# Writing out the order of the first tiles: the opening of a four-stage transformer kernel on one Trainium2 core

## The chip, the cores and the metric

The kernel runs on one NeuronCore of a Trainium2 chip. A core has engines that work side by side, each through its own instructions in order: TensorE (PE in the profile; PEld is its weight load), VectorE (DVE), ScalarE (ACT), GpSimd (POOL) and SyncE (SP), which here only starts transfers. They signal each other with semaphores. The metric is the device time in microseconds of one execution, taken as the median of several runs.

## The reference

The computation has four stages over 2048 tokens (8 sequences of 256) with 512 features. Each stage normalises its input, computes something and adds it to its input:

1. a retention-like attention over the context, with four heads of 128,
2. a feed-forward part with ternary weights,
3. an mLSTM attention with 16 heads,
4. a mixture of 32 experts, of which each token uses four, and a shared expert.

The change concerns the beginning of the first stage. What it computes, cut to that:

```python
Q = jnp.einsum('bshd,hde->bshe', xh, Wh)      # xh: the normalised tokens, by head
K = jnp.einsum('bshd,hde->bshe', kh, Wh)      # kh = vh: the context, by head
V = jnp.einsum('bshd,hde->bshe', vh, Wh)
scores = jnp.einsum('bshe,bthe->bhst', Q, K) / jnp.sqrt(jnp.float32(hd))
masked = scores * Dn[None, :, :, :]
A = jnp.maximum(jnp.abs(masked.sum(axis=0)), 1.0)   # summed over the sequences
O = jnp.einsum('hst,bthe->bshe', A, V)
```

The scores are summed over all eight sequences before they are used, so nothing of `A` is known until the last token has been normalised and multiplied.

## The kernel before, in words

Tokens are worked on in 16 tiles of 128 (`NT`), four tiles to a chunk of 512 (`CH`). Everything of the change lies in `layer0_attention` (L245), before the gate.

SyncE starts the loads in a fixed order (L260 to L278): the head weights `Wh`, then per chunk four tiles `x` and the turned context `ctxT`, then the other weights and the decay table `dec`.

Q and K need not be formed one by one: Q K^T per head is x (Wh Wh^T) k^T. So the kernel makes `G = Wh Wh^T` once. TensorE turns `Wh` (`transpose_blocks`, L137, into the PSUM tile `pt`), ScalarE copies the result to `WhT` (L286), TensorE multiplies it into `pG` (L289), and ScalarE copies that to `G` (L291).

For each tile i there are these steps:

- `stats(i)`: VectorE takes mean and variance (L129, L130), ScalarE the root `sd` (L321).
- `normed(i)`: VectorE takes the reciprocal (L325) and writes `xn` (L327), TensorE transposes it in four blocks into `pt` (L137), ScalarE copies them to `xnT` (L329).
- `values(b, j)`: TensorE multiplies context and `Wh` into `pv` (L299), ScalarE copies it to `v` (L304). This is called for the first four half sequences here, and for the rest later.
- `queries(c, h)`: TensorE multiplies a chunk of `xnT` by `G` into `pq` (L333), VectorE copies it to `q` (L335).
- `scores(c, h, q)`: TensorE adds q k^T to one of four PSUM sums `s0` to `s3` (L342, L343). Those sums were opened with a matmul of zeros (L315), after a memset of `zero` (L312).

`pt` (the tag "t") and `pv` (which shares its tag with `pG`) have one buffer each, so a transpose waits until the tile before was copied, and the first `pv` waits until `G` was copied. `xn` has two buffers.

The loop over n runs `stats` one tile ahead, `queries` four steps behind, `scores` five. In the steps 6 to 11 `ternary.add()` puts sums over the second stage's weights `wst` on ScalarE (L196). In this part no order is written by hand: the tile framework's scheduler places each instruction on its engine's queue. From the gate on (`gate`, L365), a block `tc.manual_schedule(engines=...)` keeps the written order for the engines that it names.

Of the kernel before, what the change touches and what calls it, by code (L numbers as in the profile page):

```python
# [19 lines left out]
F32 = mybir.dt.float32  # L20
# [10 lines left out]
P = 128  # L31
# [5 lines left out]
NT = T // P  # L37
CH = 512
NCH = T // CH
H0 = 4  # L40
HD0 = 128
# [84 lines left out]
def norm_stats(g, mv, x):  # L126

    st = g.small.tile([P, 6], F32, tag="st", name="st")
    g.nc.vector.bn_stats(st, x)  # L129
    g.nc.vector.bn_aggr(mv, st)  # L130


def transpose_blocks(g, pool, src, n, dtype, ident, tag):

    pt = pool.tile([P, n, P], dtype, tag=tag, name="pt")
    for k in range(n):
        g.nc.tensor.transpose(pt[:, k, :], src[:, k * P : (k + 1) * P], ident)  # L137
    return pt
# [106 lines left out]
def layer0_attention(g, tc, cp, qpool):  # L245


    nc = g.nc
# [4 lines left out]
    with ExitStack() as ctx:  # L253
        wp = ctx.enter_context(tc.tile_pool(name="a0w", bufs=1, reuse_waits="tile"))
        work = ctx.enter_context(tc.tile_pool(name="a0work", bufs=2, reuse_waits="tile"))
        ps = ctx.enter_context(tc.tile_pool(name="a0ps", bufs=1, space=PSUM, reuse_waits="tile"))


        Wh = wp.tile([P, H0, HD0], F32, tag="Wh", name="Wh")
# [22 lines left out]

        WhT = work.tile([P, H0, HD0], F32, tag="wyT", name="WhT")
        nc.scalar.copy(WhT, transpose_blocks(g, ps, Wh.rearrange("p h e -> p (h e)"), H0, F32, g.ident, "t"))  # L286
        pG = ps.tile([P, H0, HD0], F32, tag="pv", name="pG")
        for h in range(H0):
            nc.tensor.matmul(pG[:, h], lhsT=WhT[:, h], rhs=WhT[:, h], start=True, stop=True)  # L289
        G = wp.tile([P, H0, HD0], F32, tag="G", name="G")  # L290
        nc.scalar.copy(G, pG)  # L291

        V = {}

        def values(b, j):
            c, o = divmod(b * S + j * P, CH)
            pv = ps.tile([P, D], F32, tag="pv", name="pv")
            for h in range(H0):
                nc.tensor.matmul(  # L299
                    pv[:, h * HD0 : (h + 1) * HD0], lhsT=g.ctxT[c][:, h, o : o + P], rhs=Wh[:, h, :],  # L300
                    start=True, stop=True,
                )
            vj = work.tile([P, D], F32, tag=f"v{j}", name=f"v{j}")
            nc.scalar.copy(vj, pv)  # L304
            V.setdefault(b, []).append(vj)
# [3 lines left out]


        zero = work.tile([P, S + P], BF16, tag="zero", name="zero", bufs=1)
        nc.vector.memset(zero, 0.0)  # L312
        sums = [ps.tile([P, S + P], F32, tag=f"s{h}", name=f"s{h}") for h in range(H0)]
        for h in range(H0):
            nc.tensor.matmul(sums[h], lhsT=zero[:, :P], rhs=zero, start=True, stop=False)  # L315

        def stats(i):
            mv = g.small.tile([P, 2], F32, tag="mv", name="mv")
            norm_stats(g, mv, g.X[i])
            sd = g.small.tile([P, 1], F32, tag="sd", name="sd")  # L320
            nc.scalar.activation(sd, mv[:, 1:2], AF.Sqrt, bias=g.eps["ln"])  # L321
            return mv, sd

        def normed(i, mv, sd):
            nc.vector.reciprocal(sd, sd)  # L325
            xn = work.tile([P, D], F32, tag="y", name="xn")
            nc.vector.tensor_scalar(xn, g.X[i], mv[:, 0:1], sd, ALU.subtract, ALU.mult)  # L327
            c, o = divmod(i * P, CH)
            nc.scalar.copy(xnT[c][:, :, o : o + P], transpose_blocks(g, ps, xn, KD, F32, g.ident, "t"))  # L329

        def queries(c, h):
            pq = ps.tile([P, CH], F32, tag="pq", name="pq", bufs=2)
            nc.tensor.matmul(pq, lhsT=G[:, h, :], rhs=xnT[c][:, h, :], start=True, stop=True)  # L333
            q = work.tile([P, CH], F32, tag="wy", name="q")
            nc.vector.tensor_copy(q, pq)  # L335
            return q

        def scores(c, h, q):
            for o in range(0, CH, S):
                last = c == NCH - 1 and o == CH - S  # L340
                k = g.ctxT[c][:, h, o : o + S]
                nc.tensor.matmul(sums[h][:, :S], lhsT=k[:, :P], rhs=q[:, o : o + S], start=False, stop=False)  # L342
                nc.tensor.matmul(sums[h][:, S:], lhsT=k[:, P:], rhs=q[:, o + P : o + S], start=False, stop=last)  # L343

        of, q = {0: stats(0)}, {}
        for n in range(NT + H0 + 1):
            if n + 1 < NT:
                of[n + 1] = stats(n + 1)  # L350
            if n < NT:
                normed(n, *of.pop(n))
            if 0 <= n - H0 < NT:
                q[n - H0] = queries(*divmod(n - H0, H0))
            if 0 <= n - H0 - 1:
                scores(*divmod(n - H0 - 1, H0), q.pop(n - H0 - 1))
            if n < 4:
                values(*divmod(n, 2))
            elif 6 <= n < 12:
                ternary.add()  # L360
# [61 lines left out]
        po, y, pw, wy, wyT, pz, raw = ({} for _ in range(7))  # L422
        E_ = mybir.EngineType
# [1382 lines left out]
@with_exitstack  # L1806
def layers_kernel(ctx: ExitStack, tc: tile.TileContext, args):
    g = Ctx()
    g.nc = tc.nc
    for name, ap in args.items():  # L1810
        setattr(g, name, ap)
    setup(g, ctx, tc)
    dr = ctx.enter_context(tc.tile_pool(name="dram", bufs=1, space=DRAM))
    g.vc_d = dr.tile([T, D], F32, tag="vc_d", name="vc_d")

    g.h_d = dr.tile([T, D + E], F32, tag="h_d", name="h_d")
    g.parts_d = dr.tile([2, 3, P, S], BF16, tag="parts_d", name="parts_d")
    with tc.tile_pool(name="ctxT", bufs=1, reuse_waits="tile") as cp, ExitStack() as both:
        with tc.tile_pool(name="wq", bufs=1, reuse_waits="tile") as qp:
            layer0_attention(g, tc, cp, qp)  # L1820
            sp = ctx.enter_context(tc.tile_pool(name="f1early", bufs=1, side="right", reuse_waits="tile"))
            load_early(g, sp)
            wp = both.enter_context(tc.tile_pool(name="a1w", bufs=1, side="right", reuse_waits="tile"))
            gates = Gates(g, wp)
            layer1_constants(g, wp)
            layers_joined(g, tc, qp, gates)
    layer1_ffn(g, tc)
# [60 lines left out]
```

## Time and profile before

| what | value |
|---|---|
| median of 3 runs | 1054.01 us (1052.76 to 1054.70) |
| the profiled execution's own time | 1053.98 us |
| its span | 1051.8 us |
| TensorE busy | 998.3 us, 95% |
| VectorE, ScalarE, GpSimd busy | 532.3, 404.9, 394.3 us |
| first matmul of the loop over tiles (transpose of tile 0) | at 11.64 us |
| first matmul of the gate | at 60.36 us |

In lines of the timeline the first number is the start in microseconds from the span's start, the second the length; then engine, line, operation, output and inputs by the program's names with their shapes, and the count of instructions merged into the row. In brackets stand the engine's idle time before the row and what ended it. A line of the table by stretch has the stretch, its length, TensorE's busy time with the count of instructions, the granted clock as a share of full speed, the share of the DMA engines and their GB/s.

### The profile page before, as it was taken

What the parts mean: (1) busy time and instruction counts of PE and PEld (TensorE: products, weight loads), DVE (VectorE), ACT (ScalarE), POOL (GpSimd) and SP (SyncE); (2) the same over time, 40 slices, a digit from 0 to 9 for tenths busy, and PEclk for the clock granted to TensorE, in tenths of its full rate; (3) what the DMA queues carried; (4) which work ended last, traced back from release to release, by engine and by line L of the source; (5) the groups of instructions that cost most, each with busy time, mean ns of one, the idle gap of its engine ahead of it and who ended that gap; (6) DMA issues with size and microseconds to landing.
All of it is one profiled execution on the core that took longest, in us unless ns stands there. A gap on an engine that the chain in (4) does not pass through costs nothing.

```text
span 1051.8 us, 14757 instructions
## 1 busy us (share of the span) xinstructions
PE 998.3 (95%) x5210; PEld 607.5 (58%) x5210; DVE 532.3 (51%) x1417; ACT 404.9 (38%) x692; POOL 394.3 (37%) x452
## 2 busy tenths in 40 slices
PE   6999999979999899998998999999999999999994
PEld 5766666534444356665443445556666667778772
DVE  6546566679997768787828942112112121212120
ACT  4453443447687757876321001221222222221211
POOL 0023443450000114888203045554555556454522
PEclk9999999999999999999899999999999999999997
DMA  9663433323421411241112447777777778899972
GB/s 344 229 208 135 142 108 136 110 56 60 72 57 39 90 38 48 69 137 39 50 60 91 160 145 194 176 194 189 190 206 208 204 210 231 215 246 236 245 192 36
DMA packets 101011, 152.41 MB, mean 145 GB/s; under 512 B 39576, under 2 KB 42264, under 8 KB 100892
## 3 DMA queue, kind: packets, MB, share of 16 engines
q1 hardware_dynamic: 81984, 106.78, 32.4%
q0 software_dynamic: 18944, 44.60, 19.2%
q8 instruction: 43, 0.70, 0.3%
q14 instruction: 40, 0.33, 0.1%
HBM read 110.42 MB, written 32.96 MB: 136 GB/s over the span
## 4 chain that ended last, share of the span: by engine, by line
PE 74%; DVE 13%; POOL 4%; ACT 3%; issue 3%; DMA 1%; SPq 0%; POOLq 0%; DVEq 0%; ACTq 0%
PE po L1638 14%; PE pg L1621 13%; PE pu L1621 13%; PE pw L365 5%; PE pz L400 5%; PE pt L1678 3%; PE p L1118 2%; PE pgu L990 2%; DVE ct L779 2%; PE py L1165 2%; DVE h L1131 1%; PE pv L299 1%; DVE am L1135 1%; PE s L342 1%; PE pq L333 1%
## 5 line engine op out<-in xcount | busy, mean ns | idle before, releaser
L1626 DVE TENSOR_TENSOR act<-pu,sg 128x264 f32<-128x264 f32 (+22 forms) x68 | 31.9, 469 | 313.2 <-PE pu L1621 313.2
L1663 POOL DMA_INDIRECT xg<-h_d,tok_of x85 | 83.4, 981 | 197.9 <-DVE of L1673 64.8
L1682 POOL DMA_INDIRECT out_x<-eo,to x85 | 133.0, 1564 | 55.1 <-ACT eo L1720 34.4
L1638 PE MATMUL po<-w,act 128*128 128x512 f32 (+10 forms) x456 | 143.1, 489 | 0.0
L1621 PE MATMUL pg<-xT,w 128*128 128x216 f32 (+21 forms) x512 | 134.8, 406 | 0.8 <-issue 0.8
L1720 ACT ACTIVATE eo<-po,slotw 128x512 f32<-128x512 f32 (+10 forms) x114 | 65.6, 576 | 177.0 <-PE po L1638 170.6
L1621 PE MATMUL pu<-xT,w 128*128 128x216 f32 (+21 forms) x512 | 133.3, 403 | 0.0
L1621 PEld LDWEIGHTS pg<-xT,w 128*128 128x128 f32 x512 | 93.2, 190 | 33.2 <-issue 17.8
L1621 PEld LDWEIGHTS pu<-xT,w 128*128 128x128 f32 x512 | 96.8, 190 | 26.2 <-issue 5.6
L1625 ACT ACTIVATE sg<-pg 128x264 f32<-128x264 f32 (+22 forms) x68 | 28.5, 419 | 202.9 <-PE pg L1621 178.8
L1118 PE MATMUL p<-wq,xqT 128*128 128x512 bf16 (+1 forms) x384 | 81.2, 361 | 7.0 <-DVE qi L1139 6.2
L1638 PEld LDWEIGHTS po<-w,act 128*128 128x128 f32 (+10 forms) x456 | 54.2, 154 | 57.4 <-issue 47.9
L386 POOL TENSOR_TENSOR y<-y,gam 128x512 f32<-128x512 f32 x16 | 20.2, 1265 | 138.8 <-DVE y L83 138.8
L1118 PEld LDWEIGHTS <-xqT 128*128 128x128 bf16 x384 | 37.2, 98 | 49.4 <-issue 12.5
L1679 DVE TENSOR_TENSOR xT<-pt,nw 128x512 f32<-128x512 f32 (+12 forms) x85 | 51.1, 601 | 20.5 <-PE pt L1678 20.5
L400 PE MATMUL pz<-wo,wyT 128*128 128x512 f32 x128 | 59.5, 609 | 1.3 <-ACT wyT L395 1.3
L365 PE MATMUL pw<-wg,xnT 128*128 128x512 f32 x128 | 57.8, 594 | 0.0
L1678 PEld LDWEIGHTS pt<-ident,xg 128*128 128x128 f32 (+15 forms) x340 | 39.1, 140 | 23.9 <-PE po L1638 10.5
L129 DVE BATCH_NORM_STATS2 st<-x 128x6 f32<-128x512 f32 x64 | 43.9, 686 | 12.0 <-POOL x L848 6.3
L1678 PE MATMUL pt<-ident,xg 128*128 128x128 f32 (+15 forms) x340 | 47.2, 260 | 0.7 <-DVE xT L1679 0.6
L779 DVE SCALAR_TENSOR_TENSOR ct<-pqk,xe 128x768 f32<-128x768 f32 x44 | 40.0, 951 | 8.4 <-PE pqk L775 7.9
L1165 PE MATMUL py<-wq,hq 128*128 128x512 bf16 x176 | 42.3, 391 | 1.7 <-DMA hq<-hq 1.7
(336 smaller groups left out, 1680.7 us busy)
## 6 DMA issues: line engine op xcount, KB each, us to landing
w<-in_w SPq DMA_DIRECT2D x32, 1024.0 KB
w<-in_w SPq DMA_DIRECT2D x32, 512.0 KB
wst<-in_w1T SPq DMA_DIRECT2D x8, 704.0 KB
wst<-in_w3T SPq DMA_DIRECT2D x8, 704.0 KB
wst<-in_w2T SPq DMA_DIRECT2D x6, 768.0 KB
x<-in_x SPq DMA_DIRECT2D x16, 256.0 KB
ctxT<-in_ctxT_d SPq DMA_DIRECT2D x4, 1024.0 KB
raw<-in_ctx SPq DMA_DIRECT2D x16, 256.0 KB
```

The costliest lines, as they stand in the source:

```text
L365: nc.tensor.matmul(pw, lhsT=xnT[c][:, k, o : o + P], rhs=wg[:, k, :], start=k == 0, stop=k == KD - 1)
L400: nc.tensor.matmul(pz[i], lhsT=wyT[i][:, k, :], rhs=wo[:, k, :], start=k == 0, stop=k == KD - 1)
L779: nc.vector.scalar_tensor_tensor(ct[:, r : r + 2, :], pqk[:, :, : S + P], 1.0 / math.sqrt(HD1), xe[:, r : r + 2, :], ALU.mult, ALU.mult,)
L1118: nc.tensor.matmul(both[:, m, : z - a], lhsT=xqT[:, k, :], rhs=w[:, k, a:z], start=k == 0, stop=k == KD - 1)
L1165: nc.tensor.matmul(py[t], lhsT=hqT[t][0][:, f, :], rhs=w2[:, f, :], start=f == 0, stop=f == NF - 1)
L1621: nc.tensor.matmul(pp[:, :n], lhsT=w[:, k, cols], rhs=xT[:, k, :n], start=k == 0, stop=k == KD - 1)
L1638: nc.tensor.matmul(po[h * at : h * at + n, :cols], lhsT=act[:, m, j * P : j * P + n], rhs=w[:, m, h * cols : (h + 1) * cols], start=m == 0 ...
L1663: nc.gpsimd.indirect_dma_start(out=xg[:n], out_offset=None, in_=h_d, in_offset=bass.IndirectOffsetOnAxis(ap=g.tok_of[:n, r, j : j + 1], ax ...
L1678: nc.tensor.transpose(pt[:, k, :n], xg[:n, k * P : (k + 1) * P], g.ident[:n, :n])
L1679: nc.vector.tensor_mul(xT, pt[:, :, :n], g.nw.unsqueeze(2).to_broadcast([P, KD, n]))
L1682: return nc.gpsimd.indirect_dma_start(out=g.out, out_offset=bass.IndirectOffsetOnAxis(ap=rows, axis=0), in_=eo, in_offset=None, compute_op ...
L1720: nc.scalar.activation(eo[:n, at : at + cols], po, AF.Copy, scale=w[r][:n, j : j + 1])
```

## The change

The memset, the zeroing matmuls, the making of `G`, the statistics and transposes of tiles 0 to 3 and the first two `values` are taken out of the scheduler's hands: they stand in a `manual_schedule` block for TensorE, ScalarE and VectorE, one tile after another. In this block `WhT` is copied before any root is taken, and `G` after the first tile's `xnT`. The loop starts at n = 2 and keeps what is left.

```diff
-        WhT = work.tile([P, H0, HD0], F32, tag="wyT", name="WhT")
-        nc.scalar.copy(WhT, transpose_blocks(g, ps, Wh.rearrange("p h e -> p (h e)"), H0, F32, g.ident, "t"))
-        pG = ps.tile([P, H0, HD0], F32, tag="pv", name="pG")
-        for h in range(H0):
-            nc.tensor.matmul(pG[:, h], lhsT=WhT[:, h], rhs=WhT[:, h], start=True, stop=True)
-        G = wp.tile([P, H0, HD0], F32, tag="G", name="G")
-        nc.scalar.copy(G, pG)
...
         zero = work.tile([P, S + P], BF16, tag="zero", name="zero", bufs=1)
-        nc.vector.memset(zero, 0.0)
         sums = [ps.tile([P, S + P], F32, tag=f"s{h}", name=f"s{h}") for h in range(H0)]
-        for h in range(H0):
-            nc.tensor.matmul(sums[h], lhsT=zero[:, :P], rhs=zero, start=True, stop=False)
+        WhT = work.tile([P, H0, HD0], F32, tag="wyT", name="WhT")
+        G = wp.tile([P, H0, HD0], F32, tag="G", name="G")
...
-        of, q = {0: stats(0)}, {}
-        for n in range(NT + H0 + 1):
-            if n + 1 < NT:
+        of, q = {}, {}
+        E_ = mybir.EngineType
+        with tc.manual_schedule(engines={E_.PE, E_.Activation, E_.DVE}):
+            nc.vector.memset(zero, 0.0)
+            for h in range(H0):
+                nc.tensor.matmul(sums[h], lhsT=zero[:, :P], rhs=zero, start=True, stop=False)
+            nc.scalar.copy(WhT, transpose_blocks(g, ps, Wh.rearrange("p h e -> p (h e)"), H0, F32, g.ident, "t"))
+            of[0] = stats(0)
+            pG = ps.tile([P, H0, HD0], F32, tag="pv", name="pG")
+            for h in range(H0):
+                nc.tensor.matmul(pG[:, h], lhsT=WhT[:, h], rhs=WhT[:, h], start=True, stop=True)
+            normed(0, *of.pop(0))
+            nc.scalar.copy(G, pG)
+            of[1] = stats(1)
+            normed(1, *of.pop(1))
+            values(0, 0)
+            of[2] = stats(2)
+            normed(2, *of.pop(2))
+            values(0, 1)
+            of[3] = stats(3)
+            normed(3, *of.pop(3))
+        for n in range(2, NT + H0 + 1):
+            if 3 <= n < NT - 1:
                 of[n + 1] = stats(n + 1)
-            if n < NT:
+            if 3 < n < NT:
                 normed(n, *of.pop(n))
```

In the program that it builds to, the order on SyncE and GpSimd is the same as before. On TensorE two places differ: the transposes of tile 1 stand in front of the first `pv`, and the third `pv` in front of the transposes of tile 3. ScalarE has one instruction more: an activation table load in front of `WhT`, before the one in front of the first root. ScalarE's sums over `wst` stand between the copies of tiles 12 to 15, where they came earlier or later before.

## The prediction

> **What bounds the kernel now.** I read the page's engine totals and chain first, then the timelines of TensorE, ScalarE and VectorE over the first 60 us, then busy time and granted clock by stretch.
>
> ```profile
> PE 998.3 (95%) x5210; PEld 607.5 (58%) x5210; DVE 532.3 (51%) x1417; ACT 404.9 (38%) x692; POOL 394.3 (37%) x452
> ...
> PE 74%; DVE 13%; POOL 4%; ACT 3%; issue 3%; DMA 1%; SPq 0%; POOLq 0%; DVEq 0%; ACTq 0%
> ```
>
> TensorE is busy for 95% of the span and carries 74% of the chain. What comes early or late before TensorE runs without a gap is therefore handed on to the end; DMA holds 1% of the chain, so nothing there waits to swallow it. The next view is TensorE's timeline (start, length, line, operation, count, and in brackets the idle time before it and what ended it).
>
> ```profile
> 3.76 1.09 PE L137 MATMUL pt<-ident,Wh 128*128 128x128 f32 x4 [0.83 <-DMA Wh<-in_Wh]
> 9.78 2.07 PE L289 MATMUL pG<-WhT 128*128 128x128 f32 x8 [4.93 <-ACT WhT L286]
> 11.64 1.06 PE L137 MATMUL pt<-ident,xn 128*128 128x128 f32 x4
> 12.87 2.08 PE L299 MATMUL pv<-Wh,ctxT 128*128 128x128 f32 x8 [0.17 <-ACT G L291]
> 14.74 1.05 PE L137 MATMUL pt<-ident,xn 128*128 128x128 f32 x4
> 15.63 1.16 PE L299 MATMUL pv<-Wh,ctxT 128*128 128x128 f32 x8
> 16.62 0.60 PE L137 MATMUL pt<-ident,xn 128*128 128x128 f32 x4
> ...
> 18.50 0.60 PE L137 MATMUL pt<-ident,xn 128*128 128x128 f32 x4
> ...
> 20.34 0.60 PE L137 MATMUL pt<-ident,xn 128*128 128x128 f32 x4
> ```
>
> I call the five transposes of `xn` T0 to T4. Their starts are 11.64, 14.74, 16.62, 18.50 and 20.34. After T4 the loop repeats every 2.60 us without a gap until the gate begins at 60.36, so T4's start is the number to predict. Two things set it: the 4.93 us before `pG`, and the slow first matmuls. A transpose takes 1.05 us until 14.74 and 0.60 from 16.62; eight passes of `pv` take 2.08 and then 1.16.
>
> ScalarE's timeline shows why `pG` waits: `WhT` stands behind four roots `sd`, of which the last waits for the fourth tile's statistics.
>
> ```profile
> 0.75 1.28 ACT L321 ACT_TABLE_LOAD   x1 [0.75 <-PEq L1876]
> 5.23 0.29 ACT L321 ACTIVATE sd<-mv,eps_ln 128x1 f32<-128x1 f32 x1 [3.20 <-DVE mv L130]
> ...
> 8.96 0.29 ACT L321 ACTIVATE sd<-mv,eps_ln 128x1 f32<-128x1 f32 x1 [0.50 <-DVE mv L130]
> 9.16 0.57 ACT L286 COPY WhT<-pt 128x512 f32<-128x512 f32 x1
> 12.05 0.30 ACT L321 ACTIVATE sd<-mv,eps_ln 128x1 f32<-128x1 f32 x1 [2.33 <-DVE mv L130]
> 12.26 0.56 ACT L291 COPY G<-pG 128x512 f32<-128x512 f32 x1
> ```
>
> The same roots run ahead of the tiles there, which is good for T1 to T4: the roots of four tiles are taken by 9.25, before TensorE wants the first. Last, TensorE's busy time and granted clock in four stretches of 3.41 us.
>
> ```profile
> 8.83:12.24 3.41, 2.46 (x11) 1.00 1.04 396
> 12.24:15.65 3.41, 3.24 (x16) 1.00 1.06 391
> 500.34:503.76 3.42, 2.52 (x17) 0.50 0.22 81
> 503.76:507.17 3.41, 3.41 (x11) 0.50 0.00 0
> ...
> 504.55 1.06 PE L877 MATMUL hT<-ident,yn 128*128 128x128 f32 x4
> ```
>
> At a granted 0.50 four transposes take 1.06 us, as T0 does, so the first 15 us ran at half clock although the column says 1.00 there. The clock rose after a stretch with 3.24 or 3.41 us of busy TensorE, and did not after 2.46 or 2.52. Fragmented work keeps it low.
>
> **The change part by part.** Handing from engine to engine costs 0.03 to 0.06 us in these rows (`WhT` ends at 9.73, `pG` starts at 9.78).
>
> *`WhT` in front of the roots.* The transposes of `Wh` end at 4.85 as before, `WhT` takes 4.89 to 5.46, `pG` 5.51 to 7.58: 4.27 us earlier. `pG` then waits for nothing and nothing waits for it but `G`.
>
> *A second table load.* In the built program a copy is now ScalarE's first operation and gets a table load of its own; the load for the root stands behind `WhT`, since it is a different set. It takes 1.28 us, with 0.02 before and 0.01 after it (one at 550.03 follows a result that ends at 550.02). It cannot be passed on an engine that works in order, so nothing excludes its full price: 5.48 to 6.76. Then sd0 0.30, reciprocal 0.15, `xn` 0.55 and handovers: T0 at 7.9, that is 3.7 us early. Price between 0 (if the order of loads were hidden) and 1.3 on T0; I take 1.3.
>
> The Trainium skill ("ScalarE: Activation LUTs", What ACT_TABLE_LOAD costs) puts a switch of sets at 1.28 us plus a drain of 1.38, which speaks against this change. The row at 561.90 shows the next activation 0.01 us after the load, with no drain; by the page's figure the forecast would be an estimated 1.4 us higher than mine.
>
> *The written ring.* On ScalarE the order becomes WhT, sd0, xnT0, G, sd1, xnT1, v, sd2, xnT2, v, sd3; on VectorE statistics, reciprocal and `xn` of a tile now stand together, so a root is not taken ahead any more. Each tile's root waits for the copies of the tile before. That is a wait added, and behind it on ScalarE stand every later copy, on VectorE every later statistic, on TensorE the next transpose. With the durations above:
> - T0 7.9 to 8.97, xnT0 to 9.6, G to 10.06 (the two overlap by 0.1), sd1 to 10.3, reciprocal and `xn` to 11.0: T1 at 11.1 (3.6 early).
> - `pv` of the first values follows T1 at 11.95. Its data are there: tile 4, loaded behind them, reached VectorE at 11.11. At half clock its result comes at 13.87; copy to 14.5, sd2 to 14.7, another 0.8 to `xn`: T2 at 15.5 (1.1 early). TensorE has idled for about 1.8 us.
> - Second `pv` 16.4 to 18.3, its copy to 18.9, then the third `pv` 19.0 to 20.8, which now stands in front of T3: T3 at 20.8 (2.3 late). sd3 and `xn` are hidden under that third `pv`.
> - The copy of the third values ends at 21.6, the fourth `pv` starts at 21.7.
>
> *The clock.* On the stretches of the profile, 12.24 to 15.65 now holds only about 1.8 us of work and 15.65 to 19.07 about 2.75. The last is 0.80 of the stretch; the rows bound the trigger between 0.74 and 0.95. If 0.80 is not enough, the clock rises at 22.48, T4 starts at 23.0, which is 2.65 us late. If it is, V and T run fast from 19.07 and T4 starts near 21.1: 0.8 late. With no rise at all before T4 it is 24.3: 4.0 late. From T4 both kernels run the same rows at the same 2.60.
>
> I do not know that the stretches lie the same way in every execution. Moving them through all positions with the same steps, T4 comes 2.6 to 4.4 us later than before's own T4, mean 3.5, if the trigger lies above 0.80; and between 0.1 earlier and 2.8 later, mean 1.5, if below. I take 3.2, between the profile's position and the mean, as the higher trigger is nearer to the only rows that fired (0.95 and 1.00).
>
> The Trainium skill ("TensorE: Matmul & The Clock Gate", What's actually happening) says that the gate looks at free-running windows of about 3.4 us and opens after a busy one. The four rows agree with the length; that the position is free no run here shows. By the page alone, with a fully busy window wanted, the mean of 3.5 would be the forecast.
>
> *Order of the later work.* ScalarE's sums of `wst` now stand between the copies of tiles 12 to 15. Each takes 1.57 us (1.38 and a read of 0.19), and TensorE has 1.4 us of slack per copy: one copy runs from 40.60 to 41.18, and the next transposes, which want its buffer, start at 42.56. The first two loads are there long before 43.68; the third comes about 4.2 us after the first sum ends, near 46.3, the fourth near 49, both before the copies behind them are due. I cost this at nothing; without that cover 0 to 1 us. The head's zeroing matmuls, the memset, and the queues of SyncE and GpSimd keep their order: 0.
>
> Sum: 1053.98 (the profiled execution, span 1051.8 and 2.2 around it; 0.03 under the median of the runs) + 3.2 = 1057.2 us.
>
> **Rivals.**
> - *Clock rises early, ring mostly hidden* (0.0 to 1.5 late): 0.80 of a stretch suffices. For: no row between 0.74 and 0.95 excludes it. Against: nothing fired below 0.95. 1054.0 to 1055.5, say 1054.8.
> - *Faster*: the mechanism is the 4.3 us gained on `pG`, kept through to T4. It decides if sd1 to sd3 do not wait for the copies in front of them, so that TensorE's own work is the only limit after 7.9: four transposes of 0.85 and four `pv` of 1.71 at half clock put T4 at 18.2, at full clock from 12.24 at 15.2, so about 17. Price 3 us: 1051. Against it stands the order itself: v copies in front of sd2 and sd3. It wins only if T3 starts before 18.50.
> - *The ring and a late stall*: the `wst` sums hold up the last copies by up to 1 us, or the table load drains: 1058 to 1059.
>
> **How the numbers follow.** Forecast (ring with a late clock, +2 to +4.4) 0.66; early clock 0.20; faster 0.05; ring and stall 0.09. A measurement of this kernel tells about 0.2%, 2.1 us. Slower by more: nine tenths of the forecast's 0.66, all of the 0.09, and a quarter of the early-clock case where the position is bad: 0.74. Faster 0.04. The rest, 0.22, is within. The range runs from the early-clock case's middle less half the spread of the runs shown (1052.76 to 1054.70) up to the stall case: 1054.2 to 1059.2.
>
> **What would show it.** `pG` near 5.5, a table load at about 5.48 in front of the first root, T1 near 11, an idle of 1.5 to 2 us before T2, T3 behind the third `pv` near 20.8 and T4 at 22.4 to 24.3; transposes of 1.05 us as late as T2 or T3; the gate 2 to 4 us later than 60.36, and the rest of the trace the same rows shifted. A T4 before 20.3, or T2's matmuls at 0.60 us, would prove me wrong, as would a gain or loss born after 62 us.

## The result, and the profile after

The changed kernel takes 1057.34 us (median of 15 runs, 1053.01 to 1058.28); the kernel before took 1054.01 us beside it (15 runs, 1051.73 to 1056.70). The ratio is 1.0027 with a 95% interval of 1.0018 to 1.0036: slower by 0.27%, or 3.3 us. The profiled execution took 1056.78 us, 2.80 more than before's; its span is 1054.8.

The page's engine totals and chain:

```profile
PE 1000.8 (95%) x5210; PEld 610.3 (58%) x5210; DVE 532.2 (50%) x1417; ACT 406.7 (39%) x693; POOL 394.2 (37%) x452
...
PE 70%; DVE 16%; POOL 5%; ACT 3%; issue 3%; DMA 1%; DVEq 0%; POOLq 0%; ACTq 0%
```

The 5210 matmuls are the same, but TensorE is busy for 2.5 us more (998.3 before). ScalarE has one instruction more, and 4 points of the chain have gone from TensorE, most of them to VectorE. TensorE's timeline of the changed kernel shows where:

```profile
3.74 1.09 PE L137 MATMUL pt<-ident,Wh 128*128 128x128 f32 x4 [0.81 <-DMA Wh<-in_Wh]
5.50 2.08 PE L348 MATMUL pG<-WhT 128*128 128x128 f32 x8 [0.67 <-ACT WhT L344]
7.99 1.08 PE L137 MATMUL pt<-ident,xn 128*128 128x128 f32 x4 [0.40 <-DVE xn L318]
11.30 1.09 PE L137 MATMUL pt<-ident,xn 128*128 128x128 f32 x4 [2.23 <-DVE xn L318]
12.18 1.91 PE L291 MATMUL pv<-Wh,ctxT 128*128 128x128 f32 x8
15.91 1.09 PE L137 MATMUL pt<-ident,xn 128*128 128x128 f32 x4 [1.82 <-DVE xn L318]
16.79 1.92 PE L291 MATMUL pv<-Wh,ctxT 128*128 128x128 f32 x8
19.38 2.08 PE L291 MATMUL pv<-Wh,ctxT 128*128 128x128 f32 x8 [0.68 <-ACT v L296]
21.25 1.06 PE L137 MATMUL pt<-ident,xn 128*128 128x128 f32 x4
22.13 1.83 PE L291 MATMUL pv<-Wh,ctxT 128*128 128x128 f32 x8
23.80 0.60 PE L137 MATMUL pt<-ident,xn 128*128 128x128 f32 x4
...
63.82 1.02 PE L376 MATMUL pw<-wg,xnT 128*128 128x512 f32 x2
```

`pG` starts at 5.50 instead of 9.78 and T0 at 7.99 instead of 11.64. Then each tile's `xn` is late: 2.23 us of idle time stand in front of T1 and 1.82 in front of T2. T2 starts only 0.71 us before its old place, T3 2.75 us behind it and T4 at 23.80, 3.46 late. Slow transposes (1.06 us) and slow `pv` (1.8 to 1.9 us) now start as late as 21.25 and 22.13; before, the clock rose at 15.65. The gate starts at 63.82, 3.46 late too: between T4 and the gate both kernels run the same work without a gap.

ScalarE's timeline of the changed kernel has the cause of the idle times:

```profile
0.75 1.28 ACT L344 ACT_TABLE_LOAD   x1 [0.75 <-PEq L1887]
4.87 0.58 ACT L344 COPY WhT<-pt 128x512 f32<-128x512 f32 x1 [2.84 <-PE pt L137]
5.47 1.28 ACT L312 ACT_TABLE_LOAD   x1
6.76 0.29 ACT L312 ACTIVATE sd<-mv,eps_ln 128x1 f32<-128x1 f32 x1
...
14.13 0.58 ACT L296 COPY v<-pv 128x512 f32<-128x512 f32 x1 [1.12 <-PE pv L291]
14.61 0.30 ACT L312 ACTIVATE sd<-mv,eps_ln 128x1 f32<-128x1 f32 x1
```

The second table load delays the first root to 6.76. The root of tile 2 (14.61) follows the copy of `v` (14.13), which waits for the `pv` that TensorE has just done; T2 waits for that root. TensorE and ScalarE take turns. How much of the delay is idle time and how much is slow work is read from TensorE's busy time by stretch (stretch, length, busy with the count of instructions, clock, DMA share, GB/s). Before, from the transposes of `Wh` to T4:

```profile
3.76:20.34 16.58, 10.95 (x61) 1.00 1.02 373
```

After, the same work, and two stretches of 3.41 us at its end:

```profile
3.74:23.80 20.06, 14.26 (x61) 1.00 1.02 377
...
16.74:20.15 3.41, 2.73 (x13) 1.00 1.05 387
20.15:23.56 3.41, 3.41 (x17) 1.00 1.06 389
```

The same 61 instructions took 14.26 us instead of 10.95. The idle time is 5.80 us (20.06 less 14.26) instead of 5.63. So of the 3.48 us more up to T4, 3.31 are matmuls at half clock and 0.17 are idle time. The change took away one idle time of 4.93 us, and nearly the same time came back in pieces between the tiles. With the work in pieces the clock came up later: after the stretch with 2.73 us of work (0.80 of it) it did not rise, after the full one it did, at 23.56 (15.65 before).

### The profile page after: what moved, and what is told of

It is laid out like the page before. It is cut to its first block, busy times and chain, and to the rows that moved or that the text cites. A ratio compares the mean times of both kernels' runs of the same rounds, so it can differ in the third digit from the quotient of the medians.

```text
span 1054.8 us, 14764 instructions
## 1 busy us (share of the span) xinstructions
PE 1000.8 (95%) x5210; PEld 610.3 (58%) x5210; DVE 532.2 (50%) x1417; ACT 406.7 (39%) x693; POOL 394.2 (37%) x452
## 4 chain that ended last, share of the span: by engine, by line
PE 70%; DVE 16%; POOL 5%; ACT 3%; issue 3%; DMA 1%; DVEq 0%; POOLq 0%; ACTq 0%
PE po L1649 14%; PE pg L1632 12%; PE pu L1632 12%; PE pw L376 5%; PE pz L411 5%; PE pt L1689 3%; PE p L1129 2%; PE pt L137 2%; PE pv L291 2%; DVE am L1146 2%; DVE h L1142 2%; DVE ct L790 2%; DVE st L129 1%; PE s L333 1%; PE pq L324 1%
```

## The experiments

Theory A is that of the prediction: the written order makes each tile's root wait for the copies of the tile before, so TensorE works in pieces and the clock comes late. Rival B: the second table load is the loss. Rival C: the third `pv` in front of T3 is. Ratios are to the kernel before, run on the same chip.

Rival C rests on a misreading, which stands in "The change" and in the prediction too. The third `pv` stood in front of T3 before as well:

```profile
17.51 1.16 PE L299 MATMUL pv<-Wh,ctxT 128*128 128x128 f32 x8 [0.29 <-ACT v L304]
18.50 0.60 PE L137 MATMUL pt<-ident,xn 128*128 128x128 f32 x4
```

The two places that differ on TensorE are these: T1 stood behind the first `pv` and T2 behind the second, and each now stands in front of it.

### The changed kernel once more

> The changed kernel itself, on the chip of this comparison: 2 to 4 us slower than the kernel before (ratio 1.002 to 1.004). In its profile pG near 5.5, idle times of about 2.2 and 1.8 us in front of tile 1's and tile 2's transposes; the clock not up before 20 us; the gate between 62.3 and 64.3.

Measured: 1056.79 us (10 runs, 1053.41 to 1057.68), ratio 1.0030 (1.0019 to 1.0042). In its profile T4 starts at 24.07, the clock rises at 24.13 and the gate is at 64.13. The loss is there again, at the same place. The same program had its clock rise at 23.56 in one execution and at 24.13 in the other.

### The root's table set loaded first

```diff
         with tc.manual_schedule(engines={E_.PE, E_.Activation, E_.DVE}):
+            first = g.small.tile([P, 1], F32, tag="first", name="first")
+            nc.scalar.activation(first, g.eps["gn"], AF.Sqrt, bias=g.eps["ln"])
             nc.vector.memset(zero, 0.0)
```

> The changed kernel with a root of a constant as ScalarE's first operation, so that the root's table is loaded at 0.75 us and none stands behind WhT. Theory A (each tile's root behind the copies of the tile before, and the half clock that follows): the first transpose of xn comes only some 0.6 us earlier, near 7.4, because TensorE is at pG until 7.3; the wait rings stay, the fifth transpose stays between 22.7 and 23.3, the gate between 62.6 and 64.0, 0.2 to 0.6 us before the changed kernel's in the mean. Theory B (the second table load is the loss): 1.3 us or more come back and carry over every tile, the gate near 61 to 62.

Measured: 1055.56 us (12 runs, 1052.44 to 1057.83), ratio 1.0009 (0.9998 to 1.0020). TensorE's timeline in its profiled execution, which took 1052.44 us:

```profile
7.41 1.06 PE L137 MATMUL pt<-ident,xn 128*128 128x128 f32 x4
10.70 0.63 PE L137 MATMUL pt<-ident,xn 128*128 128x128 f32 x4 [2.23 <-DVE xn L318]
...
14.04 0.63 PE L137 MATMUL pt<-ident,xn 128*128 128x128 f32 x4 [1.82 <-DVE xn L318]
...
19.06 0.60 PE L137 MATMUL pt<-ident,xn 128*128 128x128 f32 x4
```

and its busy time by stretch:

```profile
3.74:19.06 15.32, 9.76 (x60) 1.00 1.01 370
5.49:8.91 3.42, 2.93 (x12) 1.00 1.01 359
```

Without the load in between, one stretch holds 2.93 us of work and the clock is up at 8.91. The two idle times, 2.23 and 1.82, are unchanged to the hundredth, and the idle time in all (5.56) is about that of the kernel before (5.63); yet the gate comes at 59.45, 0.91 before that kernel's. A, which wanted 62.6 or later, missed there, and so did B with 61 to 62. Up to T4 it is 4.74 us earlier than the changed kernel: 4.50 by faster matmuls (9.76 us busy against 14.26) and 0.24 by less idle time. So in these two executions 1.28 us of load cost over 4 us, nearly all of it through the clock. By the medians it is less: the ratio falls from 1.0027 and 1.0030 to 1.0009, some 2 us. Rival B holds for that part of the loss. The runs do not follow as clearly: they spread over 5.4 us in two groups (1052.4 to 1053.3 and 1055.1 to 1057.8), and the interval of the ratio just touches the changed kernel's. That the early rise is missed in the upper group would fit, but only the fastest of these runs was profiled, so this is argued, not shown.

### Roots taken one tile ahead, the table load kept

```diff
             of[0] = stats(0)
+            of[1] = stats(1)
...
-            of[1] = stats(1)
+            of[2] = stats(2)
             normed(1, *of.pop(1))
...
-            of[2] = stats(2)
+            of[3] = stats(3)
             normed(2, *of.pop(2))
             values(0, 1)
-            of[3] = stats(3)
```

> The changed kernel with statistics and root of tile i+1 written in front of the work on tile i, everything else as it is, second table load included. Theory A: the loss lies in roots that stand behind copies; transposes of xn at about 8.2, 10.0, 13.1, 15.7 and 17.9 to 18.5, the gate at 58.5 to 60.0, that is 3.8 to 5.3 us before the changed kernel and 0.4 to 1.9 before the kernel before; time about 1053. Theory B (table load, still there): the gate within 0.5 us of the changed kernel's 63.8. Theory C (the third pv in front of tile 3's transposes is the loss; that order changes here too): gate near 62.

Measured: 1050.92 us (6 runs, 1050.22 to 1052.80), ratio 0.9970 (0.9959 to 0.9982): 6 us better than the changed kernel, and better than the one before. TensorE's timeline:

```profile
10.32 1.11 PE L137 MATMUL pt<-ident,xn 128*128 128x128 f32 x4 [0.68 <-ACT xnT L320]
...
13.53 1.09 PE L137 MATMUL pt<-ident,xn 128*128 128x128 f32 x4 [0.39 <-DVE xn L318]
...
15.91 0.60 PE L137 MATMUL pt<-ident,xn 128*128 128x128 f32 x4
16.75 1.16 PE L291 MATMUL pv<-Wh,ctxT 128*128 128x128 f32 x8 [0.24 <-ACT v L296]
```

These are T1, T2, T3 and the third `pv`. In the source only the places of `stats` were changed. In the built program the third `pv` then stands behind T3 and the fourth behind T4. The kernel of "The third values behind T3" below has this same order on TensorE with the roots of the changed kernel, with its gate at 65.06 and a ratio of 1.0039. The two differ in the places of `stats`, so these and the clock that follows account for the difference (6.48 us at the gate, in one execution of each). The idle times of 2.23 and 1.82 shrink to 0.68 and 0.39, the clock is up at 15.68 with the table load still in place, and the gate stands at 58.58. This is theory A's own experiment, and it holds: with the roots one tile ahead the change is a gain.

### The idle times filled with work that nobody uses

Eleven matmuls of zeros on TensorE, in front of T1 (five), T2 (five) and the third `pv` (one):

```diff
             nc.scalar.copy(G, pG)
             of[1] = stats(1)
+            for _ in range(5):
+                nc.tensor.matmul(spare, lhsT=zero[:, :P], rhs=zero, start=True, stop=True)
             normed(1, *of.pop(1))
...
```

> The changed kernel with 11 more matmuls of zeros (128x384, bf16, about 0.32 us each at half clock) in the gaps of TensorE: five in front of tile 1's transposes, five in front of tile 2's, one in front of tile 3's part. They compute nothing that is used. Theory A with its clock step: TensorE is busy through a stretch of 3.41 us early, the clock rises between 9 and 15.5 us, pv takes 1.0 to 1.2 us instead of 1.9, fifth transpose at 19 to 20.5, gate at 59.1 to 61.4. If the clock has no part in it and the rings alone hold the tiles, the gate stays at 63.8 or comes later. If matmuls of zeros do not count as work for the clock, likewise.

Measured: 1055.90 us (9 runs, 1053.96 to 1060.14), ratio 1.0023 (1.0010 to 1.0036). By stretch:

```profile
11.15:14.56 3.41, 3.13 (x14) 1.00 1.05 386
219.36:226.19 6.83, 6.15 (x10) 0.50 0.38 104
233.01:236.43 3.42, 2.81 (x9) 0.50 0.00 1
```

The zeros bring nothing earlier by themselves: up to T2 every start is 0.13 or 0.14 us later than in the changed kernel, as the transposes of `Wh` are. Still the clock rises at 14.56 instead of 23.56 and the gate stands at 61.09, 2.73 us earlier than in the changed kernel: the matmuls' own slowness was that share of the 3.46. (T4 came at 21.07, 0.6 later than expected.) At the end little of it is left. At 219 us and again at 233 the clock fell in this execution, and the lag behind the kernel before grew from 0.7 to 4.0 us there, and stood near 2 us at the end. The share of the clock is shown at the gate and not in the time.

### The root's table set first, and four matmuls of zeros around the transposes of Wh

```diff
+            for _ in range(2):
+                nc.tensor.matmul(spare, lhsT=zero[:, :P], rhs=zero, start=True, stop=True)
+            ptw = transpose_blocks(g, ps, Wh.rearrange("p h e -> p (h e)"), H0, F32, g.ident, "t")
+            for _ in range(2):
+                nc.tensor.matmul(spare, lhsT=zero[:, :P], rhs=zero, start=True, stop=True)
+            nc.scalar.copy(WhT, ptw)
```

> The changed kernel with the root's table set loaded first, as in the run of that name, and four matmuls of zeros by zeros on TensorE, two in front of the turning of Wh and two behind it; their results go into a spare buffer and are used by nothing, so they add no more than TensorE's work in time in which it idled. The idle times in front of the second and third tile stay (2.23 and 1.82 us). If the clock's share is what separates the changed kernel from the kernel before, the clock is up between 5 and 9 us in this one, the gate stands at 58.6 to 61 us (before: 60.36, changed: 63.82) and the time is at or below the kernel before's, ratio 0.998 to 1.001. If the written ring by itself is the loss, the gate stays above 61.5 us and the time 1.5 us or more above before's.

Measured: 1055.55 us (12 runs, 1050.75 to 1057.98), ratio 1.0008 (0.9993 to 1.0022); the gate at 60.17. By stretch:

```profile
3.25:6.66 3.41, 3.18 (x13) 1.00 0.90 295
6.66:10.08 3.42, 1.19 (x9) 1.00 1.04 395
10.08:13.49 3.41, 2.79 (x12) 0.50 1.05 388
```

The clock rises at 6.66, as asked. The idle time in front of T1 then leaves 1.19 us of work in the next stretch (0.35), the clock falls back to 0.50 at 10.08 and rises again at 13.49. Gate and ratio are where the clock's share puts them, though the median is 1.2 us above the 1054.38 of the kernel before and not at or below it. The waiting order did harm twice here: it keeps the clock from rising, and takes it away again. The runs spread over 7.2 us here, and over 2.6 with the roots one tile ahead; that the falling clock is the cause of it was not shown.

### The third values behind T3

```diff
             normed(3, *of.pop(3))
+            values(1, 0)
...
-            if n < 4:
+            if n == 3:
```

> The changed kernel with one order undone: the third pv behind tile 3's transposes again. Theory A: tile 3's root still stands behind the copy of the second values, so TensorE only waits elsewhere: tile 3's transposes at about 20.0 to 20.5 instead of 21.3, the third pv then behind them, the gate between 62.9 and 64.9, that is within 1 us of the changed kernel. Theory C (this swap is the loss): the gate near 61 to 61.5, the time within 1 us of the kernel before.

Measured: 1057.12 us (6 runs, 1056.36 to 1057.99), ratio 1.0039 (1.0026 to 1.0051). TensorE's timeline:

```profile
20.53 1.09 PE L137 MATMUL pt<-ident,xn 128*128 128x128 f32 x4 [1.81 <-DVE xn L318]
21.41 1.91 PE L291 MATMUL pv<-Wh,ctxT 128*128 128x128 f32 x8
```

With the third `pv` out of its way, T3 waits for its root just as T2 did, 1.81 us, and comes 0.72 earlier only; the clock rises at 25.38 and the gate is at 65.06, later than the changed kernel's and 0.2 beyond the expected band. Rival C falls: in front of T3, where the kernel before had it too, the third `pv` covers a wait. No run put the first and second `pv` back in front of T1 and T2 with the roots left as they are, so what those two places add to the loss was not tested. The run with the roots one tile ahead keeps them and gains, so without the waiting roots they do not make the change a loss.

### WhT in front of the roots, and nothing else

The kernel before, with ScalarE's order alone written out, and only for `WhT` and the first tile's root:

```diff
-        of, q = {0: stats(0)}, {}
+        with tc.manual_schedule(engines={mybir.EngineType.Activation}):
+            nc.scalar.copy(WhT, transpose_blocks(g, ps, Wh.rearrange("p h e -> p (h e)"), H0, F32, g.ident, "t"))
+            of = {0: stats(0)}
```

> The kernel before with one part of the change: on ScalarE alone WhT is written in front of the first root, all else is left to the scheduler. WhT should run near 4.9, a second table load behind it, pG near 5.5. Theory A: pG's early end is worth nothing by itself, since nothing waits for it; the scheduler puts the statistics of tile 4 (data at 11.1) in front of xn of tile 0, so the first transpose comes near 13.2, the gate at 61.3 to 62.3, 1 to 2 us later than before. Against it (pG is the bound and each us it is early is won): the gate 3 to 4 us earlier than 60.4.

Measured: 1055.98 us (11 runs, 1055.10 to 1056.54), ratio 1.0012 (1.0003 to 1.0021). TensorE's timeline:

```profile
5.61 2.07 PE L345 MATMUL pG<-WhT 128*128 128x128 f32 x8 [0.68 <-ACT WhT L341]
13.63 1.08 PE L137 MATMUL pt<-ident,xn 128*128 128x128 f32 x4 [5.95 <-DVE xn L319]
```

`pG` is early and the 4.93 us in front of it are gone, but the scheduler then put the statistics of tile 4, whose data come at 11.47 here, in front of the first `xn`. T0 starts at 13.63, 2.0 later than before, and the gate at 62.86. Both are some 0.5 us later than theory A expected. This half of the change earns nothing by itself: what follows `pG` must be brought forward as well.

### One tile ahead in every step, and the root's set first

Here `normed` is split: `scaled` is VectorE's part (reciprocal, `xn`), `flipped` the transposes and the copy to `xnT`. A tile's root and `xn` stand in front of the copies of the tile before.

```diff
+            first = g.small.tile([P, 1], F32, tag="first", name="first")
+            nc.scalar.activation(first, g.eps["gn"], AF.Sqrt, bias=g.eps["ln"])
...
+            of[1] = stats(1)
+            flipped(0, xn.pop(0))
             nc.scalar.copy(G, pG)
+            xn[1] = scaled(1, *of.pop(1))
+            of[2] = stats(2)
+            flipped(1, xn.pop(1))
             values(0, 0)
+            xn[2] = scaled(2, *of.pop(2))
```

> A version meant to beat both: the root's table first (as in e1), and a written order in which a tile's root and normalisation stand in front of the tile before's copies, with the first tile's normalisation in front of the second tile's statistics. Theory A: transposes of xn near 7.4, 9.1, 11.4 to 12.3, 13.3 to 15.1, 15.3 to 17.1, no idle over 1 us among them; clock up between 8.9 and 16; gate 56.5 to 57.9, some 3 us before the kernel before; time near 1051, 0.2 to 0.4% faster. If the written order as such were the loss, it would lie near the changed kernel's time.

Measured: 1051.01 us (12 runs, 1049.80 to 1053.30), ratio 0.9978 (0.9970 to 0.9987): better than both kernels, but no better than the roots one tile ahead alone (0.9970). T4 starts at 15.67, but the gate only at 58.73, after an idle time of 1.94 us without which it would stand near 56.8. TensorE's, ScalarE's and VectorE's timelines, in this order:

```profile
57.32 0.70 PE L339 MATMUL s<-q,ctxT 128*128 128x256 f32 x2 [1.94 <-DVE q L332]
```

```profile
54.39 1.38 ACT L196 ACTIVATE wst<-wst 128x1408 f32<-128x1408 f32 x1 [1.64 <-DMA wst<-in_w3T]
...
55.76 0.92 ACT L454 ACTIVATE dec<-dec 128x384 f32<-128x384 f32 x2
```

```profile
56.30 0.36 DVE L456 TENSOR_SCALAR dec<-dec 128x384 f32<-128x384 f32 x1 [2.50 <-ACT dec L454]
56.58 0.68 DVE L332 COPY q<-pq 128x512 f32<-128x512 f32 x1
```

The sixth `wst` sum waits on ScalarE for its load until 54.39. Behind it stand the absolute values of `dec`, for which VectorE's maximum waits 2.50 us; behind that stands the copy of `q`, for which TensorE waits 1.94 us. The sums that the prediction costed at nothing do stall, once TensorE is early enough.

### The last sum behind the dec loop

```diff
-            elif 6 <= n < 12:
+            elif 6 <= n < 11:
                 ternary.add()
...
+            ternary.add()
             ternary.load_next()
             ternary.load_next()
```

> The kernel before with the order one tile ahead and the root set first, as in the run of that name, but the sixth wst sum and the two loads behind it are written behind the dec loop instead of inside it. If the sum waiting for its load at 52.7 to 54.4 us held ScalarE's abs of dec, and through VectorE's max and the copy of q the matmul at 57.3 us, the 1.94 us in front of that matmul go and the first gate matmul starts at 56.0 to 57.8 us, some 1 to 2 us earlier than in that run (58.73). By the same shift the time is 1049 to 1050.5 us, a ratio of 0.995 to 0.997 to before. Rival: what holds the matmul is the load itself or VectorE's own work; then the idle time stays above 1 us and the gate stays at 58.5 to 59. Second rival: the gain at the gate does not last to the end, since the next stretches at half clock fall elsewhere; then the gate is early and the time within 0.5 us of that run's 1051.0.

Measured: 1050.71 us (5 runs, 1050.27 to 1051.83), ratio 0.9960 (0.9946 to 0.9974), with the kernel before at 1054.38 beside it. TensorE's timeline, and then ScalarE's:

```profile
57.36 0.38 PE L340 MATMUL s<-q,ctxT 128*128 128x128 f32 x2
57.58 3.60 PE L388 MATMUL pw<-wg,xnT 128*128 128x512 f32 x8
```

```profile
58.37 0.52 ACT L452 ACTIVATE dec<-dec 128x384 f32<-128x384 f32 x1 [0.79 <-DVE dec L451]
58.80 1.36 ACT L196 ACTIVATE wst<-wst 128x1408 f32<-128x1408 f32 x1
```

The sum now runs behind `dec`, TensorE has no gap in front of the gate, and the gate starts at 57.58: 1.15 us earlier, although the clock rose 4.5 us later in this execution (13.82 against 9.29). So the chain from the load to `q` is the cause of that stall. The median lies 0.2 us above the expected band, the ratio within it: 0.4% under the kernel before, and 0.7% under the changed one by the two ratios. It is the lowest ratio of the study, but its interval overlaps those of the two other orders that run ahead, and the median is within 0.5 us of the 1051.01 without it, as the second rival said. So the gain is shown at the gate and not in the time.

### The same order with six matmuls of zeros

Added to the kernel with everything one tile ahead, four in front of T1 and two in front of T2:

> e6 with six more matmuls of zeros (nothing uses them) in TensorE's gaps: four in front of tile 1's transposes, two in front of tile 2's. Theory A: the clock rises by 12 us wherever the stretches lie, so the spread between executions shrinks; gate 56.5 to 57.0, 0 to 1.3 us before e6, 0.6 in the mean. Against it: fillers delay real work or the clock ignores them, then it is no faster than e6.

Measured: 1051.35 us (12 runs, 1049.01 to 1056.07), ratio 0.9983 (0.9967 to 0.9998). The clock was up at 9.43 with the zeros and at 9.29 without; they bring nothing, and the runs spread more, not less. The gate stood at 59.35, not at 56.5 to 57.0 as expected: T4 came 0.46 us later than without the zeros (16.13 against 15.67), and the wait for `q` was there again, with 2.10 us.

## Why the prediction was right

It said 1057.2 us, and 1057.34 was measured. The mechanism held: each tile's root waited for the copies of the tile before, and the clock came late for it. That the figures meet to 0.14 us is partly luck: 3.2 was a choice between 2.65 and 3.5, T4 came 3.46 late in one execution of the changed kernel and 3.73 in the other, and the profiled executions of the two kernels lie 2.80 apart. Point by point:

- *`pG` 4.27 earlier, at 5.51*: 5.50.
- *The second table load, 1.3 us on T0, with no drain*: it stood at 5.47 to 6.75, the root began at 6.76, T0 at 7.99 (7.9 predicted). The Trainium skill's drain of 1.38 us ("ScalarE: Activation LUTs", What ACT_TABLE_LOAD costs) is not in this trace. The start of T0 was right, the price was not: with the load taken away T0 came 0.58 us earlier (7.41) and not 1.3, since `pG` holds TensorE until then, while the gate moved by 4.4 us (63.82 to 59.45), since the clock rose early. The prediction costed the load and the clock one by one, not what the one does to the other.
- *The ring*: T1 11.1 against 11.30, idle time of 1.8 against 1.82 before T2, T2 15.5 against 15.91, T3 20.8 against 21.25, behind the third `pv`. That the third `pv` "now" stands there is a misreading (it did before, at 17.51), but the times do not rest on it. The mechanism holds, shown by the roots one tile ahead. The tenths add up from T1 (0.2 late) and from the step from tile 2's root to T2, taken as 0.8 and measured as 1.0 (14.91 to 15.91).
- *T4 between 22.4 and 24.3, the gate 2 to 4 us late*: 23.80 and 3.46. The estimate of 3.5 over all positions of the stretches, should the trigger lie above 0.80, was nearer than the 3.2 taken.
- *The clock*: the trigger was bounded to 0.74 and 0.95. A stretch with 0.80 did not raise it here, as the forecast took it. The case of a low trigger, kept at 0.20, was a fair doubt: 0.86 raised it in the experiments, and once 0.80 did (below).
- *The `wst` sums at nothing*: right here; the third and fourth sum began at 47.50 and 50.13, as soon as their loads were there (46.3 and 49 reckoned), but TensorE was busy for all of 24.23 to 63.82. The "0 to 1 us without that cover" was too low: with T4 at 15.67 it was 1.94.
- *No gain or loss born after 62 us*: not quite. The distance to the kernel before, from one matmul to the same one, is 3.45 us up to 200 us, then lies between 1.85 and 3.92 (with short swings beyond), and is 3.11 at the last matmuls. The reason is the stretches at half clock: at 360 us the kernel before has one and the changed kernel none, at 607 us it has 3.41 us of them and the changed kernel 6.83.
- *The rival "faster"* did not happen, for the reason given: the copies of `v` stand in front of the roots. Its price was sound: 3 us were named for roots that do not wait, and 3.2 were measured (0.9970).
- *The rival of the early clock* (1054.0 to 1055.5) did not decide the median. Two of the 15 runs took 1053.01 and 1053.89; whether those are its cases was not profiled.
- *The range*: by the words given for it the lower end would be 1053.8 (1054.8 less half of 1.94), not 1054.2, and the stall case ends at 1059, not at 1059.2. The measured time lies well inside either way.

## What to carry to other kernels

Count the idle time before a stage and after a change as a whole, and then in which pieces it lies: here 5.63 and 5.80 us are nearly the same, and with the pieces the matmuls took 3.3 us more, at half clock. Pieces need not cost that: with the root's table loaded first, 5.56 us in pieces went with an early clock, since one stretch was filled to 0.86 first. A written order should take the small result that the next tile waits for (here a root of 0.3 us) in front of the large copies of this one; the same edit with `stats` one tile ahead gained 3 us where the change lost 3. And when a stage moves earlier, look again at what stood comfortably behind a load: the next wait was 1.9 us long and three engines away.

## What the runs showed of the hardware

- Over all the profiled executions, up to 620 us, the granted clock never rose after a stretch of 3.41 us in which TensorE was busy for less than 0.80 of it (it did not after 0.72, 0.74, 0.77), and rose after every one with 0.87 or more. Between the two it did either: not after 0.80 in the changed kernel, and not after 0.86 at 607 us in the same execution, but after 0.85 at 505 us, and after 0.80 and 0.82 in the experiments. So the share of busy time alone, as the profile models it, does not decide there; what else counts was not tried. This is the lowest that did, in the kernel with every step one tile ahead (clock up at 9.29):

```profile
5.88:9.29 3.41, 2.73 (x13) 1.00 1.04 386
```

- The stretches do not begin with the program: the clock rose at 23.56 and 24.13 in two executions of the changed kernel, which is 0.57 us apart. The Trainium skill ("TensorE: Matmul & The Clock Gate", What's actually happening) calls the windows free-running and wants a busy one; the first agrees, and a window of 0.80 to 0.86 was sometimes enough here.
- What is won at the gate is not always won at the end. Between the gate and 620 us the clock fell to 0.50 for five stretches of 3.41 us in three of the profiled executions, six in seven (the kernel before and the changed one among them), seven in one and eight in one. From the gate to the end, taken from each profiled execution's own time and against the kernel before, the executions with five gained 1.6, gained 1.2 or stayed level; those with six lay between 0.7 gained and 1.2 lost; that with seven lost 1.0 and that with eight 3.1. The last is the kernel with six matmuls of zeros (two of its extra stretches):

```profile
231.30:234.71 3.41, 3.19 (x10) 0.50 0.11 23
367.83:371.24 3.41, 3.20 (x22) 0.50 0.25 50
```

  What decides whether the clock falls there in an execution was not tried. It makes single profiled times differ by some us in stretches whose code the experiments did not touch, so a gain at the gate is read here from traces and a gain in time from medians.
